# A graph layer on one core: the loop over units taken two at a time

## The chip, the cores and the metric

One core of a Trainium2 chip. The metric is the device time of one execution in microseconds (us); of several executions the median is given. Matrix products run on TensorE (PE; PEld is its weight load), elementwise work and reductions on VectorE (DVE), activations and copies on ScalarE (ACT), the issue of indirect gathers on GpSimd (POOL) and most other DMAs on SyncE (SP). PE writes its results to PSUM, which has eight banks.

## What is computed

```python
h = max(layernorm(x), 0)                     # x: 6250 nodes x 64
msg = relu(h[src] + edge_attr)               # 206250 edges x 64, sorted by dst
agg = segment_sum(msg, dst, 6250)
out = x + relu((h + agg) @ W1 + b1) @ W2 + b2
```

## The kernel before, in words

The edges are taken in groups of 768: 128 partitions with 6 columns each, one column being one edge per partition. There are 268 whole groups and a tail. A group's edge rows come by DMA (`attr_load`, tile `ea`). The rows `h[src]` come in two ways. Three columns of most groups are gathered on POOL, one indirect DMA per column (`gather`, L198, tile `xg`). The other three columns are a *unit*: they are fetched by matrix products. One group in 23 ("whole") has both halves fetched by products and no gather, so that it makes two units. The main loop has 276 units; two units are a *set*, and there are 138 sets.

For a set, three things are prepared and used:

- `found` and `backs`, zero-one matrices that DVE makes by comparisons (`find`, L446, three per set; `back`, L465, five per set; a sixth part of `backs` is made on ACT by `back_far`, L455, and `back_near`, L458). They need `sources` and `spots`, broadcast into SBUF by SP (`source_load`, `spot_load`).
- *Slots*: `slots_of` (L478) multiplies `found` with `hp`, the table of `h` rows split in three bf16 parts, into a PSUM tile `half` (three buffers, a bank each). `slots_out` (L486) copies it on ACT to `picked`. Six such fills, 104 matmuls, make a set.
- *Picks*: `pick` (L493, 18 matmuls per unit) multiplies `backs` with `picked` into one of two PSUM tiles, `pick_banks[u % 2]`. `room` (L499) has ACT copy the unit's edge columns beside them first.

`messages(u)` then adds gathered rows to edge rows on DVE (L560), which is the last reader of that `xg` buffer, sums a unit's four parts from PSUM into `ea` (L563) and applies relu on ACT (L565, tile `msg`). `one_hot` (L544) compares each edge's place in its window of 32 nodes. `window_sum` (L575) multiplies `msg` with it into a spare part of `pick_banks[u % 2]`, and `sum_into_z` (L538) adds that to `z`, the node table, on DVE.

Besides, once per six units, eight small steps rank the edges of a later chunk (`rank_at`, L272; `rank_count`, L277 and L279 on PE; `rank_of`, L285 to L291; `rank_marks`, L299; `rank_turn`, L315 on PE; `rank_holds`, L303; `rank_fits`; `source`, L329 on PE). Each unit has at most a few of them. Blocks of finished nodes go through W1 and W2 behind the loop (`hidden`, `result`, `store`).

The order on each engine is the order of the calls, written by hand; there is no scheduler. `half(u)` is one step of the loop. It does the window sum of unit u - 1, room for u + 1, three fills of slots for the next set, the picks of u + 1, the addition to `z` of u - 2, the messages and one-hots of u, and about half of a set's comparisons. The picks of a step go to the other `pick_banks` tile than the addition to `z` of that step reads:

```python
        if u + 1 < U:
            pick(u + 1, range(H))
        sum_into_z(u - LAG)
        blocks_behind(u - LAG)
        messages(u)
```

The rank steps of one chunk are a step of the loop apart where DVE and PE hand over (`rank_at` at u + 14, `rank_count` at u + 13, and so on). The gathers stand nine groups ahead (`AHEAD`), with twelve buffers.

Of the kernel before, what the change touches and what calls it, by code (L numbers as in the profile page):

```python
# [20 lines left out]
P = 128  # L21
G = 6
# [10 lines left out]
W = 32  # L33
# [48 lines left out]
def kernel(  # L82
# [296 lines left out]

    def combine(xg, ea, n):  # L380
        nc.vector.tensor_tensor(xg[:, :n], xg[:, :n], ea[:, :n], ALU.add)
        msg = work.tile([P, G, D], F32, name="msg", bufs=3)
        nc.scalar.activation(msg[:, :n], xg[:, :n], AF.Relu)
        return msg

# [75 lines left out]
    def back(k, q0, q1):  # L461
# [5 lines left out]
        if q1 == Q:  # L467
            spots.pop(k)

    def slots_of(k, n0):  # L470
        ps = psum.tile([P, 2, 3 * D], F32, name="half", bufs=3)
        for u in range(2):
            i, q = divmod(n0 + u, Q)
            sets = BB + 1 if q == 0 else BB
            for b in range(sets):
                for j in range(J):
                    m = (b * PARTS + q * J) + j if b < BB else BB * PARTS + j
                    nc.tensor.matmul(ps[j * S:(j + 1) * S, u], found[k][:, m, i, :],  # L478
                                     hp[:, min(m, RR - 1)].rearrange("p t d -> p (t d)"),
                                     start=(b == 0), stop=(b == sets - 1))  # L480
        if n0 == 0:
            picked[k] = hot.tile([P, 2 * Q, 3 * D], BF16, name="picked")
        halves[k, n0] = ps
# [17 lines left out]
    def group_of(u):  # L501
        return UNITS[u][0] if u >= 0 else F0 + u
# [14 lines left out]
    def norm_edges(xg):  # L517
        s = work.tile([P, G], F32, name="raw_s")
        nc.vector.tensor_reduce(s, xg, AX.X, ALU.add)
        nc.vector.tensor_scalar_mul(s, s, 1.0 / D)  # L520
        nc.vector.tensor_tensor(xg, xg, s.unsqueeze(2).to_broadcast([P, G, D]), ALU.subtract)
        sq = work.tile([P, G, D], F32, name="msg", bufs=3)
        nc.scalar.activation(sq, xg, AF.Square)
        fill()
        v = work.tile([P, G], F32, name="raw_v")
        nc.vector.tensor_reduce(v, sq, AX.X, ALU.add)
        nc.scalar.activation(v, v, AF.Sqrt, bias=eps_sb, scale=1.0 / D)
        fill()
        nc.vector.reciprocal(v, v)
        nc.vector.scalar_tensor_tensor(xg, xg, 0.0, v.unsqueeze(2).to_broadcast([P, G, D]),  # L530
                                       op0=ALU.max, op1=ALU.mult)

    aggs, hots, taken, msgs = {}, {}, {}, {}
    pick_banks = [psum.tile([P, H + 1, 4, D], F32, name=f"pick{i}", bufs=1) for i in range(2)]

    def sum_into_z(u):
# [3 lines left out]
    def one_hot(u):  # L540
        g, (lo, hi) = group_of(u), span(u)
        n = hi - lo
        oh = work.tile([P, G, W], F32, name="oh")
        nc.vector.tensor_tensor(  # L544
            oh[:, lo:hi], slot[:, g * G + lo:g * G + hi].unsqueeze(2).to_broadcast([P, n, W]),
            slots.unsqueeze(1).to_broadcast([P, n, W]), ALU.is_equal)
        hots[u] = oh
# [2 lines left out]
        if g <= NG and g not in taken:  # L550
            taken[g] = loaded[g] if g < RAW else load(g)

    def messages(u):
        g, (lo, hi) = group_of(u), span(u)
        ea, xg = taken[g]
        m = pool_cols(g)
        if g < RAW:
            norm_edges(xg)
        if m:
            nc.vector.tensor_tensor(ea[:, lo:m], ea[:, lo:m], xg[:, lo:m], ALU.add)  # L560
        if u >= 0:
            c0 = UNITS[u][1]
            nc.vector.tensor_reduce(ea[:, c0:c0 + H], picks.pop(u)[:, :H].rearrange("p j t d -> p j d t"), AX.X, ALU.add)  # L563
        msg = work.tile([P, G, D], F32, name="msg", bufs=3)
        nc.scalar.activation(msg[:, lo:hi], ea[:, lo:hi], AF.Relu)  # L565
        msgs[u] = msg
        if is_last(u):
            taken.pop(g)

    def window_sum(u):  # L570
        (lo, hi), oh, msg = span(u), hots.pop(u), msgs.pop(u)
# [43 lines left out]

    hid, res = {}, {}

    def blocks_behind(u):
        g = group_of(u)
        for c in sorted(res):  # L620
            store(c, *res.pop(c))
        for c in sorted(hid):
            res[c] = result(c, *hid.pop(c))
        for c in range(NB):
            if READY[c] == g and is_last(u):
                hid[c] = hidden(c)

    def chunk(i, then):
# [4 lines left out]
    def is_set(k):  # L633
        return 0 <= k < KS

    def half(u):
        g = group_of(u)
        k, i = divmod(u, 2)
        first = ((0, 2), (6, 8))[i]
        later = ((4,), (10,))[i]  # L640
        now = is_set(k + 1)
        if is_first(u):
            enter(g + AHEAD)
        if i == 0:
            if is_set(k + 3):
                source_load(k + 3)
        elif is_set(k + 3):
            spot_load(k + 3)
        window_sum(u - 1)
        if u + 1 < U:  # L650
            room(u + 1)
        if now:
            for n0 in first:
                slots_of(k + 1, n0)
                slots_out(k + 1, n0)
            for n0 in later:
                slots_of(k + 1, n0)
        if u + 1 < U:
            pick(u + 1, range(H))
        sum_into_z(u - LAG)  # L660
        blocks_behind(u - LAG)
        messages(u)
        if now:
            for n0 in later:
                slots_out(k + 1, n0)
        one_hot(u)
        if i == 0:
            if is_set(k + 1):
                back_near(k + 1)
                back(k + 1, 3, Q)  # L670
            if is_set(k + 2):
                find(k + 2, 0)
                find(k + 2, BB)
        else:
            if is_set(k + 2):
                back_far(k + 2)
                back(k + 2, 0, 3)
                find(k + 2, 1)
        chunk(u + 14, rank_at)
        chunk(u + 13, rank_count)  # L680
        chunk(u + 12, rank_of)
        chunk(u + 11, rank_marks)
        chunk(u + 11, rank_turn)
        chunk(u + 10, rank_holds)
        chunk(u + 10, rank_fits)
        chunk(u + 9, source)
        if g in CHECKS and is_first(u):
            find_left(CHECKS.index(g))

    def fill():  # L690
        while split:
# [55 lines left out]
        spot_load(k)  # L747
    for g in range(F0):
        enter(g + AHEAD)
        messages(g - F0)  # L750
        one_hot(g - F0)
        if g == 0:
            rank_at(1)
# [9 lines left out]
        if g == 3:  # L763
            rank_at(2)
            rank_count(2)
        if g >= 1:
            window_sum(g - 1 - F0)
        if g > LAG:
            sum_into_z(g - LAG - 1 - F0)
# [3 lines left out]
    ln_stack.close()  # L773
    hot = ctx.enter_context(tc.tile_pool(name="hot", bufs=2))

    for b in range(BB + 1):
        find(0, b)
    back_far(0)
    back(0, 0, Q)
    back_near(0)  # L780
    for n0 in range(0, 2 * Q, 2):
        slots_of(0, n0)
        slots_out(0, n0)
    source_load(2)
    spot_load(2)
    room(0)
    pick(0, range(H))
    for b in range(BB + 1):
        find(1, b)
    back_far(1)  # L790
    back(1, 0, 3)
    for u in range(U):
        half(u)
    xbs[NB] = old_rows(NB)
    for c in sorted(hid):
        res[c] = result(c, *hid.pop(c))
    window_sum(U - 1)
    for c in sorted(res):
        store(c, *res.pop(c))
# [78 lines left out]
```

## Time and profile before

| | |
|---|---|
| three runs | 1760.12, 1771.63, 1772.58 us; median 1771.63 |
| the profiled execution | 1747.93 us, its span 1746.2 us |
| granted PE clock, mean | 0.907 |
| busy: PE, PEld, DVE, ACT, POOL | 1302.7, 991.3, 1024.7, 871.5, 802.7 us |
| slots, L478 PE | 14352 matmuls, 500.8 us |
| picks, L493 PE | 4968 matmuls, 574.6 us |
| window sums, L575 PE | 3224 matmuls, 177.3 us |
| `half` to `picked`, L486 ACT | 828 copies, 477 ns each |
| reduces, L563 DVE | 276, 951 ns each |
| `backs`, L465 DVE | 690, 251.0 us |
| `found`, L446 DVE | 414, 212.4 us |
| one-hots, L544 DVE | 281, 341 ns each |
| first and last pick begin at | 114.3 and 1733.1 us |

Busy time is the time in which an engine had an instruction running; matmuls overlap each other, so that their sum can't be read as a rate. In a line of a timeline the numbers are start and duration in us, then engine, source line, operation, tiles, shapes and how many instructions were merged (x43); square brackets give the idle time of that engine before the line and what ended it, "issue" being nothing that the profile shows. In a line of groups the bar is followed by busy time, mean ns of one, and the idle time before them with its main reason.

### The profile page before, as it was taken

What the parts mean: (1) busy time and instruction counts of PE and PEld (TensorE: products, weight loads), DVE (VectorE), ACT (ScalarE), POOL (GpSimd) and SP (SyncE); (2) the same over time, 40 slices, a digit from 0 to 9 for tenths busy, and PEclk for the clock granted to TensorE, in tenths of its full rate; (3) what the DMA queues carried; (4) which work ended last, traced back from release to release, by engine and by line L of the source; (5) the groups of instructions that cost most, each with busy time, mean ns of one, the idle gap of its engine ahead of it and who ended that gap; (6) DMA issues with size and microseconds to landing.
All of it is one profiled execution on the core that took longest, in us unless ns stands there. A gap on an engine that the chain in (4) does not pass through costs nothing.

```text
span 1746.2 us, 54838 instructions
## 1 busy us (share of the span) xinstructions
PE 1302.7 (75%) x23181; PEld 991.3 (57%) x23181; DVE 1024.7 (59%) x2686; ACT 871.5 (50%) x1955; POOL 802.7 (46%) x798
## 2 busy tenths in 40 slices
PE   3047787778778778777777877877777877777787
PEld 2035566556557556565655655655665655565566
DVE  7346556546565665555755655654566566465576
ACT  4235455446455555554544544644554555454465
POOL 6734435444453553544544444444444445444430
PEclk9998889889897898989988988987899889898898
DMA  6223334334333442443433333333333334333341
GB/s 181 66 57 108 103 93 109 91 88 114 99 98 95 114 109 82 108 106 93 117 96 91 106 99 95 104 98 90 94 103 106 93 106 110 86 103 95 97 111 33
DMA packets 115095, 172.34 MB, mean 99 GB/s; under 512 B 28443, under 2 KB 83612, under 8 KB 114844
## 3 DMA queue, kind: packets, MB, share of 16 engines
q1 hardware_dynamic: 89752, 143.03, 27.4%
q0 software_dynamic: 25088, 25.74, 8.3%
q8 instruction: 184, 3.01, 0.7%
q14 instruction: 67, 0.55, 0.1%
q10 hardware_dynamic: 4, 0.01, 0.0%
HBM read 164.85 MB, written 3.84 MB: 97 GB/s over the span
## 4 chain that ended last, share of the span: by engine, by line
PE 64%; issue 18%; another core or an unknown queue 7%; ACT 6%; DVE 3%; POOL 1%; DMA 1%; DVEq 0%; ACTq 0%; POOLq 0%
PE pick L493 28%; PE half L478 24%; PE pick L575 8%; ACT picked L486 2%; PE rows L329 1%; ACT msg L565 1%; PE rows L592 1%; PE rows L603 1%; ACT dist L455 1%; PE rows L279 1%; POOL xg L198 1%; PE rows L277 1%; PE rows L315 0%; ACT backs L458 0%
## 5 line engine op out<-in xcount | busy, mean ns | idle before, releaser
L198 POOL DMA_INDIRECT xg<-h_rows,src_sb x754 | 768.0, 1019 | 865.4 <-DVE ea L560 688.2
L478 PE MATMUL half<-hp,found 128*32 128x192 bf16 x14352 | 500.8, 260 | 215.3 <-issue 191.8
L486 ACT CAST picked<-half 128x384 bf16<-128x384 f32 x828 | 381.1, 477 | 521.7 <-remote 321.7
L493 PE MATMUL pick<-picked,backs 128*128 128x192 bf16 x4968 | 574.6, 267 | 83.9 <-issue 64.2
L493 PEld LDWEIGHTS <-backs 128*128 128x128 bf16 x4968 | 446.6, 106 | 198.1 <-issue 179.6
L478 PEld LDWEIGHTS <-found 128*32 128x32 bf16 x14352 | 340.7, 100 | 320.7 <-issue 284.0
L538 DVE TENSOR_TENSOR z<-z,pick 128x32 f32 x281 | 53.1, 189 | 656.7 <-issue 236.4
L563 DVE TENSOR_REDUCE ea<-pick 128x192 f32<-128x768 f32 x276 | 262.5, 951 | 0.0
L465 DVE TENSOR_SCALAR backs<-spots,ids 128x768 bf16<-128x768 int16 x690 | 251.0, 415 | 0.0
L575 PE MATMUL pick<-oh,msg 128*64 128x32 f32 x3224 | 177.3, 237 | 54.6 <-ACT msg L565 29.5
L446 DVE TENSOR_SCALAR found<-sources,nodes_of 128x1536 bf16<-128x1536 int16 (+1 forms) x414 | 212.4, 542 | 0.1
L575 PEld LDWEIGHTS pick<-oh,msg 128*64 128x64 f32 x3224 | 138.4, 149 | 119.7 <-issue 53.7
L565 ACT ACTIVATE msg<-ea 128x384 f32<-128x384 f32 (+2 forms) x281 | 144.4, 514 | 24.5 <-DVE ea L563 12.8
L499 ACT COPY pick<-ea 128x192 f32<-128x192 f32 x276 | 88.6, 321 | 126.0 <-remote 69.4
L458 ACT ACTIVATE backs<-dist,ones 128x768 bf16<-128x768 bf16 x138 | 130.5, 946 | 0.3 <-ACT dist L455 0.3
L455 ACT ACTIVATE dist<-spots,far 128x768 bf16<-128x768 int16 x138 | 129.9, 941 | 0.0
L544 DVE TENSOR_TENSOR oh<-slot,slots 128x192 f32<-128x192 int16 (+2 forms) x281 | 95.7, 341 | 24.2 <-remote 24.2
L560 DVE TENSOR_TENSOR ea<-ea,xg 128x192 f32<-128x192 f32 x252 | 90.2, 358 | 3.4 <-issue 1.9
L277 PE MATMUL rows<-at,upper 128*128 128x432 f16 x46 | 17.0, 369 | 44.9 <-remote 24.1
L281 ACT CAST before<-rows 128x432 f16<-128x432 f32 x46 | 23.6, 514 | 48.4 <-remote 38.8
L332 ACT CAST source<-rows 24x64 int16<-24x64 f32 x138 | 27.6, 200 | 35.9 <-remote 27.6
L329 PE MATMUL rows<-holds,marks 128*96 128x96 f16 x276 | 27.6, 235 | 15.2 <-DVE oh L544 4.9
(102 smaller groups left out, 435.1 us busy)
## 6 DMA issues: line engine op xcount, KB each, us to landing
sources<-source_row SPq DMA_DIRECT2D x138, 384.0 KB
ea<-in_edge_attr_dram SPq DMA_DIRECT2D x268, 192.0 KB
spots<-spot_rows SPq DMA_DIRECT2D x138, 192.0 KB
xg<-h_rows,src_sb POOLq DMA_INDIRECT x754
xb<-in_x_dram SPq DMA_DIRECT2D x12, 128.0 KB
out_dram<-o SPq DMA_DIRECT2D x12, 128.0 KB
h_rows<-x SPq DMA_DIRECT2D x3, 384.0 KB
dst_sb<-in_dst_main_dram SPq DMA_DIRECT2D x1, 804.0 KB
```

Of the source, the lines that this page charges most:

```text
L198: nc.gpsimd.indirect_dma_start(out=xg[:, j, :], out_offset=None, in_=rows[:, :], in_offset=bass.IndirectOffsetOnAxis(ap=idx[:, j:j + 1], a ...
L446: nc.vector.tensor_scalar(found[k][:, b * PARTS:b * PARTS + n].rearrange("p m i s -> p (m i s)"), sources[k][:, :n * 2 * S], nodes_of[:, b ...
L455: nc.scalar.activation(dists[k], spots[k].bitcast(I16), AF.Abs, bias=far)
L458: nc.scalar.activation(backs[k][:, Q - 1].rearrange("p t s -> p (t s)"), dists.pop(k), AF.Relu, bias=ones[:, 0:1], scale=-1.0)
L465: nc.vector.tensor_scalar(backs[k][:, q].rearrange("p t s -> p (t s)"), spots[k].bitcast(I16), ids[:, q:q + 1], None, op0=ALU.is_equal)
L478: nc.tensor.matmul(ps[j * S:(j + 1) * S, u], found[k][:, m, i, :], hp[:, min(m, RR - 1)].rearrange("p t d -> p (t d)"), start=(b == 0), st ...
L486: nc.scalar.copy(picked[k][:, n0:n0 + 2], halves.pop((k, n0)))
L493: nc.tensor.matmul(ps[:, u, :3].rearrange("p t d -> p (t d)"), backs[k][:, q, i * H + u, :], picked[k][:, i * Q + q], start=(q == 0), stop ...
L544: nc.vector.tensor_tensor(oh[:, lo:hi], slot[:, g * G + lo:g * G + hi].unsqueeze(2).to_broadcast([P, n, W]), slots.unsqueeze(1).to_broadca ...
L563: nc.vector.tensor_reduce(ea[:, c0:c0 + H], picks.pop(u)[:, :H].rearrange("p j t d -> p j d t"), AX.X, ALU.add)
L565: nc.scalar.activation(msg[:, lo:hi], ea[:, lo:hi], AF.Relu)
L575: nc.tensor.matmul(pa[i * D:(i + 1) * D], msg[:, j, :], oh[:, j, :], start=(j < lo + 2), stop=(j >= hi - 2))
```

## The change

The step of the loop is now a set, `both(k)`, with units 2k and 2k + 1. The two window sums come first (of the set before), then the sums by node (`messages` is split in `total` and `relu`; the reduce now stands ahead of the addition of gathered rows), with room for the next set's units and six fills of slots, then two relus, the picks of both units of the next set, both additions to `z`, both one-hots, and all comparisons for the set two ahead. `msg` gets four buffers for three, `oh` four for two. The two SP loads of a set stand together. The rank steps of both units stand at the end of the step. Ahead of the loop, set 1 gets all of its comparisons and set 0 both of its picks.

```diff
+    def backs_of(k):
+        back_far(k)
+        back(k, 0, Q)
+        back_near(k)
...
-        oh = work.tile([P, G, W], F32, name="oh")
+        oh = work.tile([P, G, W], F32, name="oh", bufs=4)
...
-    def messages(u):
+    def total(u):
         g, (lo, hi) = group_of(u), span(u)
         ea, xg = taken[g]
         m = pool_cols(g)
-        if g < RAW:
-            norm_edges(xg)
-        if m:
-            nc.vector.tensor_tensor(ea[:, lo:m], ea[:, lo:m], xg[:, lo:m], ALU.add)
         if u >= 0:
             c0 = UNITS[u][1]
             nc.vector.tensor_reduce(ea[:, c0:c0 + H], picks.pop(u)[:, :H].rearrange("p j t d -> p j d t"), AX.X, ALU.add)
-        msg = work.tile([P, G, D], F32, name="msg", bufs=3)
-        nc.scalar.activation(msg[:, lo:hi], ea[:, lo:hi], AF.Relu)
-        msgs[u] = msg
+        if m:
+            nc.vector.tensor_tensor(ea[:, lo:m], ea[:, lo:m], xg[:, lo:m], ALU.add)
+        totals[u] = ea
         if is_last(u):
             taken.pop(g)
+
+    def relu(u):
+        lo, hi = span(u)
+        msg = work.tile([P, G, D], F32, name="msg", bufs=4)
+        nc.scalar.activation(msg[:, lo:hi], totals.pop(u)[:, lo:hi], AF.Relu)
+        msgs[u] = msg
...
-    def half(u):
...
+    def both(k):
+        us = (2 * k, 2 * k + 1)
+        ahead = is_set(k + 1)
+        for u in us:
+            if is_first(u):
+                enter(group_of(u) + AHEAD)
+        if is_set(k + 3):
+            source_load(k + 3)
             spot_load(k + 3)
+        for u in us:
+            window_sum(u - 2)
+        for u in us:
+            total(u)
+            if ahead:
+                room(u + 2)
+                for n0 in range(u % 2 * Q, u % 2 * Q + Q, 2):
+                    slots_of(k + 1, n0)
+                    slots_out(k + 1, n0)
+        for u in us:
+            relu(u)
+        if ahead:
+            for u in us:
+                pick(u + 2, range(H))
+        for u in us:
+            sum_into_z(u - 2)
+        blocks_behind([u - 2 for u in us])
+        for u in us:
+            one_hot(u)
+        if is_set(k + 2):
+            backs_of(k + 2)
+            for b in range(BB + 1):
+                find(k + 2, b)
+        for u in us:
+            chunk(u + 14, rank_at)
+            chunk(u + 13, rank_count)
+            chunk(u + 12, rank_of)
+            chunk(u + 11, rank_marks)
+            chunk(u + 11, rank_turn)
+            chunk(u + 10, rank_holds)
+            chunk(u + 10, rank_fits)
+            chunk(u + 9, source)
...
-    for u in range(U):
-        half(u)
+    for k in range(KS):
+        both(k)
```

## The prediction

> **What bounds the kernel now.** I read the chain of waits and the groups of instructions first, then the timeline of single units, then the order of the changed program.
>
> From the chain (first line) and the groups:
>
> ```profile
> PE 64%; issue 18%; another core or an unknown queue 7%; ACT 6%; DVE 3%; POOL 1%; DMA 1%; DVEq 0%; ACTq 0%; POOLq 0%
> ...
> L198 POOL DMA_INDIRECT xg<-h_rows,src_sb x754 | 768.0, 1019 | 865.4 <-DVE ea L560 688.2
> ...
> L538 DVE TENSOR_TENSOR z<-z,pick 128x32 f32 x281 | 53.1, 189 | 656.7 <-issue 236.4
> ```
>
> PE carries the chain, with 18% in which it waits for nothing that shows ("issue"). DVE has slack: 656.7 us of it stand ahead of the addition to z, once per unit. POOL's gathers wait for the addition of edge and gathered rows (L560), which frees their buffer.
>
> Where the 18% goes, in one unit at granted clock 1.00:
>
> ```profile
> 820.04 0.19 DVE L538 TENSOR_TENSOR z<-z,pick 128x32 f32 x1 [2.43 <-ACT msg L565]
> 820.17 0.36 DVE L560 TENSOR_TENSOR ea<-ea,xg 128x192 f32<-128x192 f32 x1
> 820.27 0.54 PE L575 MATMUL pick<-oh,msg 128*64 128x32 f32 x12
> 820.45 0.95 DVE L563 TENSOR_REDUCE ea<-pick 128x192 f32<-128x768 f32 x1
> 820.74 1.09 PE L478 MATMUL half<-hp,found 128*32 128x192 bf16 x43
> 820.80 0.94 POOL L198 DMA_INDIRECT xg<-h_rows,src_sb  x1 [1.82 <-DVE ea L560]
> 822.14 0.27 PE L478 MATMUL half<-hp,found 128*32 128x192 bf16 x2 [0.32 <-issue]
> 822.88 0.33 PE L478 MATMUL half<-hp,found 128*32 128x192 bf16 x5 [0.47 <-issue]
> 823.62 0.29 PE L478 MATMUL half<-hp,found 128*32 128x192 bf16 x2 [0.42 <-issue]
> 823.85 0.34 PE L493 MATMUL pick<-picked,backs 128*128 128x192 bf16 x2
> 824.39 0.49 PE L493 MATMUL pick<-picked,backs 128*128 128x192 bf16 x4 [0.21 <-issue]
> 825.15 1.15 PE L493 MATMUL pick<-picked,backs 128*128 128x192 bf16 x12 [0.27 <-issue]
> ```
>
> The gathers start 0.27 us after L560. Some 43 matmuls later PE falls into steps of 0.75 us with 2 to 6 matmuls each, until 0.77 us after the third gather's end (824.38). I call it the stutter: 58 matmuls from 820.80 to 825.15. The last units have no gathers left:
>
> ```profile
> 1724.19 0.54 PE L575 MATMUL pick<-oh,msg 128*64 128x32 f32 x12
> 1724.67 1.26 PE L478 MATMUL half<-hp,found 128*32 128x192 bf16 x52
> 1725.86 1.66 PE L493 MATMUL pick<-picked,backs 128*128 128x192 bf16 x18
> 1727.44 0.54 PE L575 MATMUL pick<-oh,msg 128*64 128x32 f32 x12
> ```
>
> There a unit takes 3.25 us, against (1733.4 - 114.3) / 276 = 5.87 us over the loop. So the loop is bound by PE plus the stutter. A longer burst, six gathers in a row, is in the trace too:
>
> ```profile
> 456.74 1.04 POOL L198 DMA_INDIRECT xg<-h_rows,src_sb  x1 [6.28 <-DVE oh L544]
> ...
> 463.18 0.95 POOL L198 DMA_INDIRECT xg<-h_rows,src_sb  x1 [0.30 <-issue]
> ...
> 463.97 0.29 PE L478 MATMUL half<-hp,found 128*32 128x192 bf16 x4 [1.14 <-issue]
> 465.39 0.69 PE L478 MATMUL half<-hp,found 128*32 128x192 bf16 x12 [1.14 <-issue]
> ```
>
> From 456.74 to 465.39, 8.65 us, PE gets through 68 matmuls by the timeline's counts, less than two trios pass in that time.
>
> **The change, part by part.** Counts of matmuls, comparisons, copies and gathers stay. Extra buffers (msg, oh) cost nothing in time; the prologue gains one unit's picks and part of a set's comparisons, at most 18 x 0.088 + 3 x 0.364 + 0.95 = 3.6 us. SP issues a set's two loads together, three sets ahead; they have a whole set of cover.
>
> The added wait decides. In both(k), sum_into_z(u-2) stands behind pick(u+2), and both use pick_banks[u % 2]. In the changed program as built, DVE's additions to z wait for the last matmul of pick(u+2), of the very set in hand. Before, the pick they waited for was the preceding step's. Queued behind them on DVE: two one-hots, five backs, three finds, the rank steps, then the next set's reduces and L560 additions. Who waits for that:
> - PE: the rank product (L315, L329 or L277, one per set) now follows the set's picks and waits for a DVE rank step of the same set; the next window sums and slots stand behind it.
> - ACT: room(u+2) waits for the next reduce and stands ahead of slots_out; with three half buffers PE gets through three of six banks and stops.
> - POOL: the gathers wait for the L560 additions.
>
> So a set becomes a loop. From T, the end of a set's picks, at full clock:
> 1. z 0.10 after T, 0.19; one-hots 2 x 0.341; backs 251.0 / 690 x 5 = 1.82; finds 212.4 / 138 = 1.54: T+4.3.
> 2. Rank steps, one of three kinds per set: L285, L288, L291 (0.377 + 0.603 + 0.180), L303 (0.55) or L272 (0.45), mean 0.72: T+5.0. PE's product 0.57 on average with 0.1 to start, then the first window sums 0.54 and 0.1: T+6.3.
> 3. First reduce to T+7.25; L560 ends at T+7.5; gathers from T+7.8; second reduce to T+8.4.
> 4. room 0.32, then copies 0.43 apart: the three banks are free at T+8.1, 8.5 and 8.95. PE does the other 52 slot matmuls behind them, to T+9.5.
> 5. 36 picks at 1.58 / 18 = 0.088: T+12.7.
>
> That is already more than 11.72 us per set (1617.5 / 138 from 115.9 to 1733.4). The stutter comes on top, and nothing hides it now: six gathers start at T+7.8, and steps 4 and 5 (88 matmuls) run under them. What the stutter lets through is not shown for this mix. By the burst of six it is 68 in 8.65 us, to T+16.45: 20 picks are left, 1.76 us: **18.2**. By the rate between the gaps in bursts of three (median 4.4 matmuls per us over 170 of them, counted in the timeline) it is 52 + 29 by T+16, and T+16.6. I take the first, since the burst has the same length. With one trio in a set: 58 by T+12.15 to 13.4, 24 to 30 picks left: 15.2.
>
> 754 / 3 = 252 units (rounded) have gathers, 24 have none: 114 sets of 18.2 and 24 of 15.2, mean 17.7; x 138 = 2440. With 114 us ahead of the first pick, 13 behind the last and 3.6 of prologue: 2570 against the span of 1746.2. The profiled run's whole time was 1747.93; the median of the three runs, 1771.63, is 1.0136 times that: **2600**.
>
> Clock: from 869 to 873 PE was busy 1.43 of 4.00 us, and from 873.5 to 880.5 the granted clock averaged 0.52. At half clock picks take 2.19 / 13 = 0.168 and twelve window matmuls 0.86 instead of 0.54. PE now has nothing to do from T to T+5.1. If that halves the clock each time, leftover picks cost 1.6 to 2.2 us more and a set 0.3 elsewhere: mean 19.7 per set, 2880. I keep it as the upper end, for stretches as idle as the stutter often left the clock at 1.00 (820 to 826: 1.00). The Trainium skill ("TensorE: Matmul & The Clock Gate", section on HAM oscillation) says that idle gaps over about 3.4 us put the clock to half. By that rule the sum is this 2880, and these rows agree in part.
>
> **The rivals.**
> - *The loop of waits without the stutter*: PE, having waited, holds enough ready work to get through 88 matmuls. For: it ran about 43 to 53 before the first gap. Against: 88 is more. 12.7 per set: 138 x 12.7 + 130 = 1883, x 1.0136 = 1908; with 36 picks and the window sums at half clock (2.9 + 0.3 more per set) 2360. The Trainium skill ("Runtime: NRT & Kernel Launch", section "Instruction fetch mechanics") has PE's instructions streamed ahead and hidden, which would leave no stutter: its time is this 1908. The gaps during gathers speak against it.
> - *Faster*: one burst of six falls on window sums and picks, and the 84 slot matmuls that are left run unhindered. This decides if DVE's work after the picks fits under window sums and slots, about 3.3 us, or PE needn't wait for it: 8.2 us for 80 matmuls and 84 x 0.024 = 2.0, 10.3 per set, 138 x 10.3 + 130, x 1.0136 = 1570. Against: step 1 alone is 4.3 us, and ACT's order holds three banks back.
> - *No change*: waits shrink until the old 11.7 per set returns. Nothing in the order does that.
>
> **How the numbers follow.** Forecast 0.75 (2360 to 2880), first rival 0.17 (1900 to 2360), faster 0.05, no change 0.03. Within 1% is about what a measurement of this kernel tells from none. The range goes from 1900, to hold the first rival, to 2880.
>
> **What would show it.** Right: z's idle time ended by PE's pick, and that idle before the additions, with DVE idle during picks and PE idle after them; PE's window sums or rank product ended by DVE; bursts of six gathers of 7.5 us; PE's busy share near 50%; a lower granted clock. Wrong: gaps of "issue" gone while POOL gathers (first rival), or window sums starting within 1 us of the last pick (then the loop of waits isn't there, and the time is near or below the old one).

## The result, and the profile after

| | before | after |
|---|---|---|
| median (lowest to highest), six runs each | 1763.01 us (1737.17 to 1772.58) | 2901.42 us (2897.99 to 2907.06) |
| the profiled execution, its span | 1747.93, 1746.2 us | 2904.16, 2902.4 us |
| granted PE clock, mean | 0.907 | 0.731 |
| busy: PE, DVE, POOL | 1302.7, 1024.7, 802.7 us | 1663.3, 1019.8, 747.1 us |

The ratio is 1.6601, with an interval of 1.65 to 1.6703; it is taken over the fast runs alone, which are three of the six before, so it is not the quotient of the two medians. The forecast was 2600 us with a range of 1900 to 2880, so the measured time lies 0.7% above the range's upper end, on the forecast side and by a larger amount than forecast.

Line numbers have moved: slots are now L483, picks L498, the copies to `picked` L491, the addition to `z` L543, the one-hots L549, the addition of gathered rows L566, the window sums L582. The page's busy times and groups of the changed kernel (busy us, mean ns of one, then idle time ahead of the group and what ended most of it):

```profile
PE 1663.3 (57%) x23181; PEld 1317.5 (45%) x23181; DVE 1019.8 (35%) x2686; ACT 909.0 (31%) x1955; POOL 747.1 (26%) x798
...
L198 POOL DMA_INDIRECT xg<-h_rows,src_sb x754 | 713.1, 946 | 2044.6 <-DVE ea L566 1854.3
L483 PE MATMUL half<-hp,found 128*32 128x192 bf16 x14352 | 754.5, 337 | 571.9 <-issue 520.3
...
L543 DVE TENSOR_TENSOR z<-z,pick 128x32 f32 x281 | 53.0, 189 | 1697.2 <-PE pick L498 1615.3
...
L498 PE MATMUL pick<-picked,backs 128*128 128x192 bf16 x4968 | 626.1, 305 | 17.9 <-issue 17.0
...
L315 PE MATMUL rows<-ident_b,spot_i 128*18 128x128 bf16 x46 | 12.0, 260 | 226.0 <-DVE spot_i L291 226.0
L329 PE MATMUL rows<-holds,marks 128*96 128x96 f16 x276 | 28.2, 246 | 191.0 <-DVE holds L303 182.1
L277 PE MATMUL rows<-at,upper 128*128 128x432 f16 x46 | 19.2, 418 | 201.5 <-DVE at L272 195.0
```

Of these, the page of the kernel before has:

```profile
L478 PE MATMUL half<-hp,found 128*32 128x192 bf16 x14352 | 500.8, 260 | 215.3 <-issue 191.8
L493 PE MATMUL pick<-picked,backs 128*128 128x192 bf16 x4968 | 574.6, 267 | 83.9 <-issue 64.2
...
L277 PE MATMUL rows<-at,upper 128*128 128x432 f16 x46 | 17.0, 369 | 44.9 <-remote 24.1
...
L329 PE MATMUL rows<-holds,marks 128*96 128x96 f16 x276 | 27.6, 235 | 15.2 <-DVE oh L544 4.9
```

DVE's idle time ahead of the addition to `z` went from 656.7 to 1697.2 us, and 1615.3 us of it now end with a pick. PE in turn loses 226.0 + 182.1 + 195.0 = 603 us ahead of the three rank products, each time to a DVE step; before, it stood idle there for 12.7 us (L315), 15.2 us (L329) and 44.9 us (L277), and mostly waited for something else. So the two engines wait for each other in turn, once per set. PE's other idle time is nearly all "issue" ahead of slots, 520.3 us against 191.8; picks, which had 64.2 us of it before, have 17.0.

One set of the timeline (start, duration, engine, line; square brackets: idle time before, and what ended it):

```profile
1514.86 0.19 DVE L543 TENSOR_TENSOR z<-z,pick 128x32 f32 x1 [1.28 <-PE pick L498]
...
1515.50 1.73 DVE L465 TENSOR_SCALAR backs<-spots,ids 128x768 bf16<-128x768 int16 x5
1517.14 1.34 DVE L446 TENSOR_SCALAR found<-sources,nodes_of 128x1536 bf16<-128x1536 int16 x3
...
1519.00 0.56 PE L329 MATMUL rows<-holds,marks 128*96 128x96 f16 x6 [4.24 <-DVE holds L303]
1519.49 1.40 PE L582 MATMUL pick<-oh,msg 128*64 128x32 f32 x24
...
1520.82 3.28 PE L483 MATMUL half<-hp,found 128*32 128x192 bf16 x82
...
1522.50 0.95 POOL L198 DMA_INDIRECT xg<-h_rows,src_sb  x1 [14.17 <-DVE ea L566]
...
1524.56 0.34 PE L483 MATMUL half<-hp,found 128*32 128x192 bf16 x5 [0.45 <-issue]
...
1526.73 0.37 PE L483 MATMUL half<-hp,found 128*32 128x192 bf16 x4 [0.47 <-issue]
...
1528.75 0.95 POOL L198 DMA_INDIRECT xg<-h_rows,src_sb  x1 [0.30 <-issue]
...
1529.63 0.38 PE L483 MATMUL half<-hp,found 128*32 128x192 bf16 x4 [0.39 <-issue]
...
1531.06 5.85 PE L498 MATMUL pick<-picked,backs 128*128 128x192 bf16 x36 [1.05 <-issue]
...
1537.00 0.19 DVE L543 TENSOR_TENSOR z<-z,pick 128x32 f32 x1 [2.61 <-PE pick L498]
```

Read from the first line to the last, this is the loop: the addition to `z` waits for the picks, then DVE works through comparisons while PE stands idle for 4.24 us, then window sums and slots start, then six gathers run in a row from 1522.50 to 1529.70, and PE crawls through slots in steps of one to five matmuls until 1531.06. Only then do the 36 picks of the set run, all of them, and DVE waits for their end.

The same set cut into its three stretches (columns: length, busy us of PE, PEld, DVE, ACT and POOL with instructions, granted clock, DMA share, GB/s):

```profile
1514.80:1522.50 7.70, 3.50 (x74) 3.33 (x77) 7.54 (x21) 1.08 (x5) 0.00 (x0) 0.81 0.09 19
1522.50:1531.00 8.50, 4.15 (x68) 1.92 (x61) 0.87 (x2) 1.90 (x5) 5.67 (x6) 0.70 0.62 165
1531.00:1537.00 6.00, 5.85 (x36) 5.24 (x35) 0.19 (x1) 1.69 (x4) 0.00 (x0) 0.52 0.10 33
```

In the first stretch DVE is busy nearly throughout (7.54 of 7.70 us) and PE less than half. In the second POOL gathers, DVE mostly stands, and PE is busy for half of it. In the third PE works nearly alone, at a granted clock of 0.52.

For the numbers below: on some occasions the chip showed no stutter at all, and the kernel before then took 1102 to 1104 us with all its gathers, so that a time is only to be read beside that of the kernel before in the same group. Where the changed kernel did not run in a group, its 2901.42 us stand in for it below; over the three groups in which it ran, its time differed by 1.2%.

### The profile page after: what moved, and what is told of

Its sections match the earlier page's. It is cut to its first block, busy times and chain, and to the rows that moved or that the text cites. A ratio compares the mean times of both kernels' runs of the same rounds, so it can differ in the third digit from the quotient of the medians.

```text
span 2902.4 us, 54486 instructions
## 1 busy us (share of the span) xinstructions
PE 1663.3 (57%) x23181; PEld 1317.5 (45%) x23181; DVE 1019.8 (35%) x2686; ACT 909.0 (31%) x1955; POOL 747.1 (26%) x798
## 3 DMA queue, kind: packets, MB, share of 16 engines
q1 hardware_dynamic: 89752, 143.03, 16.8%
q0 software_dynamic: 25088, 25.74, 4.7%
## 5 line engine op out<-in xcount | busy, mean ns | idle before, releaser
L198 POOL DMA_INDIRECT xg<-h_rows,src_sb x754 | 713.1, 946 | 2044.6 <-DVE ea L566 1854.3
L483 PE MATMUL half<-hp,found 128*32 128x192 bf16 x14352 | 754.5, 337 | 571.9 <-issue 520.3
L483 PEld LDWEIGHTS <-found 128*32 128x32 bf16 x14352 | 510.8, 129 | 776.7 <-issue 714.0
L543 DVE TENSOR_TENSOR z<-z,pick 128x32 f32 x281 | 53.0, 189 | 1697.2 <-PE pick L498 1615.3
L491 ACT CAST picked<-half 128x384 bf16<-128x384 f32 x828 | 374.6, 482 | 865.6 <-remote 512.0
L498 PE MATMUL pick<-picked,backs 128*128 128x192 bf16 x4968 | 626.1, 305 | 17.9 <-issue 17.0
L498 PEld LDWEIGHTS <-backs 128*128 128x128 bf16 x4968 | 568.6, 124 | 82.5 <-issue 59.2
L465 DVE TENSOR_SCALAR backs<-spots,ids 128x768 bf16<-128x768 int16 x690 | 238.7, 413 | 0.0
L582 PE MATMUL pick<-oh,msg 128*64 128x32 f32 x3224 | 189.0, 282 | 3.4 <-DVE oh L549 3.4
L446 DVE TENSOR_SCALAR found<-sources,nodes_of 128x1536 bf16<-128x1536 int16 (+1 forms) x414 | 184.6, 501 | 0.1
L582 PEld LDWEIGHTS pick<-oh,msg 128*64 128x64 f32 x3224 | 170.3, 205 | 30.9 <-issue 19.1
L315 PE MATMUL rows<-ident_b,spot_i 128*18 128x128 bf16 x46 | 12.0, 260 | 226.0 <-DVE spot_i L291 226.0
L329 PE MATMUL rows<-holds,marks 128*96 128x96 f16 x276 | 28.2, 246 | 191.0 <-DVE holds L303 182.1
L277 PE MATMUL rows<-at,upper 128*128 128x432 f16 x46 | 19.2, 418 | 201.5 <-DVE at L272 195.0
L574 ACT ACTIVATE msg<-ea 128x384 f32<-128x384 f32 (+2 forms) x281 | 129.4, 515 | 7.7 <-DVE ea L566 7.3
L329 PEld LDWEIGHTS <-marks 128*96 128x96 f16 x276 | 26.4, 158 | 199.0 <-issue 164.1
L315 PEld LDWEIGHTS <-spot_i 128*18 128x18 bf16 x46 | 4.1, 90 | 239.8 <-DVE spot_i L291 239.8
```

What stands on the lines that cost most here:

```text
L198: nc.gpsimd.indirect_dma_start(out=xg[:, j, :], out_offset=None, in_=rows[:, :], in_offset=bass.IndirectOffsetOnAxis(ap=idx[:, j:j + 1], a ...
L446: nc.vector.tensor_scalar(found[k][:, b * PARTS:b * PARTS + n].rearrange("p m i s -> p (m i s)"), sources[k][:, :n * 2 * S], nodes_of[:, b ...
L465: nc.vector.tensor_scalar(backs[k][:, q].rearrange("p t s -> p (t s)"), spots[k].bitcast(I16), ids[:, q:q + 1], None, op0=ALU.is_equal)
L491: nc.scalar.copy(picked[k][:, n0:n0 + 2], halves.pop((k, n0)))
L498: nc.tensor.matmul(ps[:, u, :3].rearrange("p t d -> p (t d)"), backs[k][:, q, i * H + u, :], picked[k][:, i * Q + q], start=(q == 0), stop ...
L574: nc.scalar.activation(msg[:, lo:hi], totals.pop(u)[:, lo:hi], AF.Relu)
```

## The experiments

Times are medians where there were several runs. Each group of kernels ran together with the kernel before on one chip, and the time of the kernel before on that chip is given beside them.

**Both kernels again.** The unedited kernels were timed on another chip, and the changed one on a further one.

> The kernel before, unchanged, run and traced once more, since beside the two runs with the late additions it took 1102 us and not 1763. If PE's stutter under gathers is a property of the kernel, 1737 to 1773 us with the gaps of issue. If it is a condition of the machine that comes and goes between loads of a program, either that, or 1102 us with gathers running and no gaps, which is the time of the kernel without gathers (1103 us).

> The changed kernel, unchanged, beside it. With the stutter about 2901 us. Without it the loop of waits through DVE alone is left, and the time is that of the changed kernel without gathers, about 1966 us, slower than the kernel before by the factor 1.78.

> The changed kernel as it is, to see its time beside a kernel before of known state. If the kernel before shows the gaps (1735 to 1765 us): 2860 to 2910. If it shows none (about 1103 us): by the theory that the loss is the loop of waits plus the gaps, about the 1966 us that it took without gathers; by the rival that gathers cost the changed kernel something of their own apart from the gaps, over 2050.

The kernel before took 1735.41 us (ratio to its companions 1.0008, 0.9958 to 1.0058), the changed one 2867.25 (1.6546, 1.6415 to 1.6676) and 2868.34 beside 1731.7. The size of the loss holds in all three groups. All three met the stutter, so the time of the changed kernel on a chip without it stays unmeasured.

**No gathers.** In both kernels the gathers of the loop are left out and a zeroed tile stands in their place; all else stays.

```diff
         else:
-            xg = edge.tile([P, G - H, D], F32, name="xg")
+            return ea, none
         gather(...)
...
+    none = const.tile([P, G - H, D], F32, name="none")
+    nc.vector.memset(none, 0.0)
```

> The changed kernel without the gathers of the main loop (a tile of zeros is added in place of the gathered rows; all else runs). Theory: the loop of waits alone is left, 12.7 us per set at full clock to 15.9 at half clock: 1880 to 2320 us, and no gaps of issue of 0.4 us and more in the slots. Rival (the stutter has nothing to do with the gathers): over 2700 us with the gaps in place.

> The kernel before without the gathers of the main loop (zeros added in place of the gathered rows). Theory: each unit takes the 3.25 us of the last units of the trace, 6.5 us per set and about 1030 us in all. Rival (the gaps of issue come from PE's own stream of instructions): 1600 us or more, gaps in place.

The changed kernel took 1965.67 us, the kernel before 1103.28 (about 1030 were expected), beside 1764.86 for the kernel before as it is. So 662 us of the kernel before are owed to its gathers (1764.86 - 1103.28), and 936 us of the changed kernel (2901.42 - 1965.67). What is left, 1965.67 - 1103.28 = 862 us, is the price of the waits, with the lower clock that goes with them (0.762 against 0.968). The timeline of the changed kernel without gathers shows them with nothing in the way:

```profile
995.70 3.14 PE L500 MATMUL pick<-picked,backs 128*128 128x192 bf16 x36
1003.77 0.22 PE L317 MATMUL rows<-ident_b,spot_i 128*18 128x128 bf16 x1 [4.92 <-DVE spot_i L293]
1003.92 1.26 PE L584 MATMUL pick<-oh,msg 128*64 128x32 f32 x24
1005.11 3.53 PE L485 MATMUL half<-hp,found 128*32 128x192 bf16 x104
1008.58 3.14 PE L500 MATMUL pick<-picked,backs 128*128 128x192 bf16 x36
```

PE is idle for 4.92 us after the picks, and then the 104 slots and 36 picks run without one gap of "issue". From pick to pick this set takes 1008.58 - 995.70 = 12.88 us, and the sets 13.6 on average. The prediction's loop without stutter has 12.7.

**The addition to `z` ahead of the picks.** One edit of the changed kernel, called the early-additions kernel below: both additions stand right behind the window sums.

```diff
         for u in us:
             window_sum(u - 2)
+        for u in us:
+            sum_into_z(u - 2)
         for u in us:
             total(u)
...
-        for u in us:
-            sum_into_z(u - 2)
```

> The changed kernel with both additions to z moved ahead of the sums by node, so that they wait for the window sums and not for the set's picks; nothing is left out. Theory (two parts: a loop of waits through DVE, and PE's stutter under a burst of six gathers): the loop is cut, DVE's comparisons fall beside slots and picks, z's idle time is no longer ended by PE's pick. The burst of six stays and starts about 2.8 us after the picks' end, so a set takes 13.2 to 15.6 us and the kernel 1950 to 2280 us, still slower than the kernel before. Rival (the loop of waits alone makes the loss): 11.7 us or less per set, 1760 us or less. Rival (the burst alone makes it): over 2700 us.

> The changed kernel with the additions to z moved ahead of the sums by node, beside it. With the stutter about 2157 us. Without it about 1276 us, its time without gathers: the loop of waits is cut, and what is left over the kernel before (1102 us) is about 174 us of waits in the middle of the slots.

It took 2156.51 us, and 2126.35 in another group (ratio 1.227, 1.2181 to 1.2359). That is 745 us less than the changed kernel's 2901.42, and 741 less than the 2867.25 that the changed kernel took beside the second: two thirds of the 1138 us that the change lost (2901.42 - 1763.01). The timeline says why:

```profile
1202.74 0.89 PE L582 MATMUL pick<-oh,msg 128*64 128x32 f32 x24
1203.56 1.26 PE L483 MATMUL half<-hp,found 128*32 128x192 bf16 x52
1205.75 1.17 PE L483 MATMUL half<-hp,found 128*32 128x192 bf16 x45 [0.94 <-ACT picked L491]
```

Window sums and slots now follow at once. What PE waits for next is the copy of a bank (`picked`), because `room` stands ahead of it on ACT and waits for DVE's reduce. Over the whole run this wait is 120.0 us; 419.5 us more are "issue" ahead of slots and picks.

The same kernel with the gathers left out as above:

> The kernel z_early without the gathers of the main loop (zeros added in place of the gathered rows). Theory: what is left of a set is PE's 6.5 us and the wait of about 0.9 us for a free half buffer in the middle of the slots, so 7.4 us per set and 1100 to 1200 us; the difference from z_early's 2157 us, about 1000 us, is then the price of 754 gathers in bursts of six, against 1764.9 - 1103.3 = 662 us for the same gathers in bursts of three. Rival (z_early is slow by some other wait in its order): over 1500 us.

1276.34 us, above what was expected. So 173 us of waits are left (1276.34 - 1103.28) that the early addition does not remove; and its gathers cost 2156.51 - 1276.34 = 880 us, against 662 us for the same 754 gathers in the kernel before.

**The rank steps moved apart.** The changed kernel, its late additions kept, with the rank steps put so that each product of PE uses a DVE step of an earlier set.

```diff
-            chunk(u + 14, rank_at)
-            chunk(u + 13, rank_count)
-            chunk(u + 12, rank_of)
+            chunk(u + 18, rank_at)
+            chunk(u + 15, rank_count)
+            chunk(u + 14, rank_of)
...
-            chunk(u + 10, rank_holds)
-            chunk(u + 10, rank_fits)
+            chunk(u + 12, rank_holds)
+            chunk(u + 12, rank_fits)
...
+        if g == 4:
+            rank_of(2)
```

> The changed kernel with the rank steps spread so that each of PE's rank products stands one set behind the DVE step that feeds it; nothing is left out. Theory (PE's window sums and slots stand behind the rank product, which waits for the end of DVE's comparisons): window sums start about 1 us after the picks' end in place of about 5, all of the first three banks of slots are done when the gathers start, about 10 more matmuls are ahead of the burst; 1.5 to 2.6 us per set less, 2540 to 2700 us. Rival (the rank product hides behind the wait for the half buffers): within 2% of the changed kernel, about 2900 us.

2498.18 us beside 1764.86: 403 us better than the changed kernel, a little more than expected, and still far from the kernel before. The rank products no longer wait, but the slots behind them do:

```profile
1221.87 1.50 PE L582 MATMUL pick<-oh,msg 128*64 128x32 f32 x24 [0.70 <-DVE oh L549]
1224.23 0.35 PE L483 MATMUL half<-hp,found 128*32 128x192 bf16 x4 [0.86 <-DVE found L446]
1224.76 2.15 PE L483 MATMUL half<-hp,found 128*32 128x192 bf16 x48 [0.18 <-DVE found L446]
```

The comparisons that the next step's slots need end only after this step's picks, because they stand behind the addition to `z`. Slots wait 150.2 us for `found` in this kernel, by its list of PE's waits, against 6.8 us in the changed one, where the wait for the rank product stands ahead and hides it.

**What in a gather makes the stutter.** The kernel before with each gather of the loop replaced by a plain DMA of as many rows, without indices, issued from POOL or from SP. The rows are the wrong ones for the sum; bytes, buffers and waits stay.

```diff
-        gather(xg[:, lo:], src_sb[:, g * G + lo:g * G + hi], hi - lo, x if g < RAW else h_rows)
+        if g < F0:
+            gather(...)
+        else:
+            for j in range(lo, hi):
+                nc.gpsimd.dma_start(out=xg[:, j, :], in_=h_rows[j * P:(j + 1) * P, :])
```

> The kernel before with each gather of the main loop replaced by a plain DMA of 128 whole rows of h (fixed rows, so the sums are other sums), still issued by POOL. Asks what of a gather makes PE stutter. If it is POOL's issue of a DMA: 1600 us or more with the gaps of issue in place. If it is the indexed form of the gather: 1100 to 1250 us without gaps.

> The same plain DMAs issued by SP in place of POOL. If the bytes moved or their landing in SBUF make PE stutter: 1600 us or more. If it is POOL's work: 1100 to 1250 us without gaps.

> The plain DMAs from POOL in place of the gathers, once more, beside kernels with gathers, as no kernel with gathers ran beside it the first time. If the indexed gathers are what PE's stutter needs: about 1100 us while the kernel before takes 1712 to 1773 us. If the traffic does it too: 1600 us or more.

From POOL 1100.39 us, from SP 1096.84, and from POOL in another group 1106.2 beside 1756.45 (0.6274, 0.62 to 0.6348). These are the times without any gather. In the kernel with POOL's plain DMAs POOL still issues 754 of them, by its groups of instructions:

```profile
L225 POOL DMA_DIRECT2D xg<-h_rows x754 | 467.3, 631 | 525.3 <-DVE ea L564 504.0
```

The DMA table of that page has the same 25088 packets and 25.74 MB on the queue of POOL's DMAs (q0) as that of the kernel with gathers. So neither the bytes nor the packets nor the issue of DMAs on POOL holds PE up. It takes the indexed gather. The plain DMAs read rows that lie side by side, so whether it is the index or the scattered rows was not separated.

**Where and how the gathers stand.** The kernel before, with the addition of gathered rows and the relu moved behind the one-hots, or behind the comparisons, so that gathers start at another place of the unit.

```diff
+    def messages_end(u):
+        ...
+        if m:
+            nc.vector.tensor_tensor(ea[:, lo:m], ea[:, lo:m], xg[:, lo:m], ALU.add)
+        msg = ...
...
         one_hot(u)
+        messages_end(u)
```

> The kernel before with the addition of gathered rows (L560) and the relu behind it moved after the unit's reduce and one-hot, so that each burst of three gathers starts about 2.0 us after the picks' end in place of 0.87, when the 52 slot matmuls of that unit are done. Nothing is left out. Theory (a burst lets through a number of matmuls, not a time of them, so it should meet the long picks and leave the short slots outside): a unit takes 5.0 to 5.3 us in place of 5.87, 1510 to 1600 us. Rival (the place of a burst in the unit does not matter): within 2% of the kernel before. Second rival (bursts run into each other and become bursts of six): slower than before.

> The same with the addition and relu moved further, after the unit's share of comparisons, so that a burst starts about 3.4 us after the picks' end. Theory: 5.0 to 5.3 us per unit, 1510 to 1600 us, as the burst now meets the window sums and part of the slots of the next unit after 43 matmuls of grace. Rival (the place does not matter): within 2% of the kernel before. Second rival (relu comes too late for the window sums, PE waits for ACT): slower than the kernel with the addition after the one-hot.

> The kernel before with the addition of gathered rows moved after the one-hot, once more, as its first runs met a machine in which the kernel before did not stutter (1102 us). If it stutters now (the kernel before at 1712 to 1773 us): by the theory that a burst lets through a number of matmuls, 1510 to 1600 us; by the rival that the burst's place in a unit does not matter, within 2% of the kernel before. If it does not stutter, 1110 us again and nothing new.

The first two met a chip without the stutter: 1110.5 us beside 1102.21 (1.0069, 1.0042 to 1.0096) and 1220.75 (1.1062, 1.1027 to 1.1098), the second because the relu comes too late for the window sums (PE waits 114.8 us for it there). On a chip with the stutter the first took 1935.43 us beside 1756.45 (1.0952, 1.0826 to 1.1079). The expected 1510 to 1600 us did not come, but the idea that a later start would let a unit's slots escape was not tried by itself, since the bursts have joined: the trace has 40 of six gathers in a row (at most 0.4 us apart) and 157 of three, where that of the kernel before has 6 and 225.

That made the number of gathers in a row the next suspect. The early-additions kernel was changed so that only the first unit's buffer comes free before the picks; the addition and the relu of the second unit stand behind the comparisons.

```diff
     def relu(u):
         lo, hi = span(u)
+        if u >= 0 and u % 2:
+            m = pool_cols(group_of(u))
+            if m:
+                ea, xg = totals[u], gathered.pop(u)
+                nc.vector.tensor_tensor(ea[:, lo:m], ea[:, lo:m], xg[:, lo:m], ALU.add)
...
-        for u in us:
-            relu(u)
+        relu(us[0])
...
             for b in range(BB + 1):
                 find(k + 2, b)
+        relu(us[1])
```

> The kernel z_early with the second unit's addition of gathered rows and relu moved after the set's comparisons, so that the six gathers of a set come as two bursts of three with a pause. With the stutter: if the loss of z_early (2126 to 2157 us) comes from bursts of six, which let through 62 to 68 matmuls where two of three let through 58 each, a set takes 10.5 to 12.5 us in place of 14.5, 1600 to 1860 us. If the number of gathers counts and not their grouping, within 2% of z_early. Without the stutter: about 1280 us.

1757.64 us beside 1756.45 (1.0039, 0.9998 to 1.008): 369 to 399 us less than the early-additions kernel (2126.35 and 2156.51), and no different from the kernel before. The trace has 237 bursts of three and none of six, where that of the early-additions kernel has 107 of six. One unit's addition and relu moved with the split, so the 369 us can't be put down to the bursts alone.

**Room behind the first copies.** The largest wait left in the kernel with the split was the one for a bank. Its list of PE's waits (instruction, what it waited for, us in all, times, longest):

```profile
PE half L483 <- ACT picked L491: 147.2, 118, 4.8
PE half L483 <- issue: 135.0, 308, 1.2
PE pick L498 <- issue: 51.7, 192, 0.7
```

The rooms were put behind the first three copies.

```diff
-            if ahead:
-                room(u + 2)
-                for n0 in range(u % 2 * Q, u % 2 * Q + Q, 2):
-                    slots_of(k + 1, n0)
-                    slots_out(k + 1, n0)
+        if ahead:
+            for n0 in range(0, 2 * Q, 2):
+                if n0 == Q:
+                    for u in us:
+                        room(u + 2)
+                slots_of(k + 1, n0)
+                slots_out(k + 1, n0)
```

> The kernel z_early_split with both rooms moved behind the first three copies of slots, so that those copies no longer wait on ACT behind a room that waits for a reduce. Nothing is left out. Theory: the wait of about 1 us for a free half buffer in the middle of the slots goes, and with the stutter a set takes 10.7 to 11.2 us in place of 11.7, 1610 to 1690 us against 1712 to 1773 us for the kernel before. Rival (the time that PE no longer waits is lost again under the burst, which lets through a fixed number of matmuls): within 2% of the kernel before. Without the stutter: about 1140 us against 1102 us.

> The kernel with the early additions to z, split bursts and both rooms behind the first three fills, once more, on whatever the kernel before does beside it. If the kernel before shows the gaps (1735 to 1765 us): z_early_split took 1757.64 there; the rooms were in the way of slots_out only while ACT waited for the second reduce, under 1 us per set, so 1650 to 1760 by the theory that ACT's order still costs something, and 1760 or more by the rival that the wait for DVE behind the picks (a rank step, 0.8 us of idle PE per set without gaps) sets the end anyway. If the kernel before shows no gaps (about 1103 us): 1282 again, within 1%.

On a chip without the stutter it took 1281.75 us beside 1103.84 (1.1643, 1.1607 to 1.1678), more than expected. On one with the stutter it took 1639.45 us beside 1731.7: ratio 0.9452, 0.9385 to 0.9519, somewhat better than the theory's lower end of 1650. Its list of PE's waits:

```profile
PE half L483 <- issue: 106.7, 257, 1.2
PE rows L315 <- DVE spot_i L291: 60.1, 37, 5.4
PE pick L498 <- issue: 48.9, 159, 1.7
...
PE half L483 <- ACT picked L491: 1.1, 4, 0.3
```

The 147.2 us for a bank are 1.1 us, and the wait for the rank step, 6.3 us with the split alone, takes back 60.1. This version beats both kernels where the stutter is present. Where it is absent it takes 16% longer than the kernel before.

## Where the prediction was right, and where it was wrong

**Right: before is bound by PE plus the stutter.** Without the gathers PE is busy for 91% of the span, with no group that has more than 1 us of "issue" ahead of slots or picks, and 662 of 1765 us go.

**Right: the added wait and the loop.** The additions to `z` wait for the set's own picks, comparisons queue behind them, and PE's rank product waits for those. Moving the additions alone took away two thirds of the loss. The signs named ahead are there: DVE idle under the picks and PE behind them, bursts of 7.2 us (1522.50 to 1529.70; 7.5 were forecast), and PE busy for 57% of the span where about 50% was forecast.

**Right in size: the loop without the stutter.** 12.7 us per set and 1908 us in all were forecast for that rival, 2360 at half clock; the kernel without gathers took 13.6 us per set and 1965.67 us in all, at a granted clock of 0.762. As a rival it fell, since the gaps stayed. The Trainium skill ("Runtime: NRT & Kernel Launch", section "Instruction fetch mechanics") has instructions streamed ahead with the fetch mostly hidden. By that the time would have been this one; the 520.3 us of "issue" ahead of slots speak against taking it as a rule for PE while POOL gathers, though no run shows that the fetch is what holds PE up.

**Wrong: the term for picks under the burst.** The prediction had 52 of a set's 104 slots done when the burst starts, held there by the banks. Of the other 88 matmuls, 68 pass in the 8.65 us from the burst's start, 52 slots and 16 picks, and 20 picks are left at 0.088 us. The trace has 106 sets with six gathers in a row (the loop's first set left out):

| from the end of a set's picks | predicted | measured, mean |
|---|---|---|
| to the first gather | 7.8 us | 7.41 us |
| first gather to the first pick | | 9.35 us |
| first pick to the end of the last | | 4.69 us |
| these two together | 8.65 + 1.76 = 10.41 us | 14.04 us |
| the set | 18.2 us | 21.45 us |

When the burst began, 28 slots had started in 97 of the 106 sets, not 52, so that 76 were still ahead. (The set shown above is one of the exceptions, with 44.) The banks did not hold them: PE's waits for `picked` ahead of slots are 1.9 us in the whole run. The slots had only just begun, and at half clock. This is the time from the first slot to the first gather in the next set (length, busy us of PE and PEld with instructions of L483, granted clock, DMA share, GB/s):

```profile
1543.55:1544.52 0.97, 0.97 (x28) 0.96 (x32) 0.50 0.77 143
```

That is 0.035 us for a slot, where the forecast reckons with 0.024. What a burst lets through was nearly right: in the median 63 matmuls start in the 8.65 us from the first gather, against 68. But they were slots. About 13 slots and all 36 picks were left behind the burst, not 20 picks, and a pick took 4.69 / 36 = 0.130 us, not 0.088. So what was left took 14.04 - 8.65 = 5.39 us where 20 x 0.088 = 1.76 were forecast, 3.63 us more; the burst starts 0.39 us earlier than forecast, and the rest is the 3.25 us by which the set is longer. At the forecast's own prices, 13 slots and 36 picks are 13 x 0.024 + 36 x 0.088 = 3.48 us, so that by this estimate about half of the miss is the count of what was left and half its lower rate.

The sets with fewer gathers were too short in the forecast as well: the 22 with three took 16.8 us where 15.2 were forecast. The six behind the last gather took 11.3 us.

**Too low: the clock.** The sum was made at full clock, with half clock as its upper end. The granted clock was 0.731 on average, 0.52 in the stretch of picks above. The Trainium skill ("TensorE: Matmul & The Clock Gate", section on HAM oscillation) ties a halved clock to idle gaps over about 3.4 us. The changed kernel has one such gap in most sets (4.24 us above), and by that rule the sum was 2880. That 2901 us are so near is in part luck, since that sum keeps the 20 picks and prices them at 0.168 us, 3.4 us in all, where 13 slots and 36 picks took 5.39. A single long gap isn't needed, either. In the kernel with the rank steps apart no idle time of PE from 1221 to 1239 us is longer than 0.9 us, and the granted clock is 0.50 throughout, by the same columns as the stretches above:

```profile
1221.00:1230.00 9.00, 6.43 (x128) 5.19 (x127) 6.97 (x18) 2.06 (x6) 1.95 (x3) 0.50 0.21 74
1230.00:1239.00 9.00, 6.87 (x39) 4.73 (x38) 0.19 (x1) 3.80 (x7) 3.71 (x4) 0.50 0.09 18
```

The traces show what does go with it. In the loop of the changed kernel the granted clock is 0.50 or 1.00 for pieces of 3.41 us: it went up only behind a piece in which PE was busy for 80% or more of the time, and down only behind one with 63% or less (247 times each). In the kernel with the rank steps apart, PE is busy for 60 to 77% of each such piece from 1222.6 to 1236.3 us, and the clock stays down. No experiment separates the clock's share of the loss from that of the gaps.

**Overlooked: the comparisons as a second wait.** The prediction put PE's wait on the rank product alone. It cost nothing in the forecast, as the rank product is the later of the two, but it made the rank steps look like the one thing to move, and moving them recovered 403 us, not the 603 that PE loses there.

**The rival on the other side** (1570 us) asked that DVE's work behind the picks fit under window sums and slots, or that PE not wait for it. Neither holds in the changed kernel: PE waits 4 to 5 us. The kernel that came near to it, with early additions, split bursts and late rooms, meets its second condition in most sets, and took 1639.45 us. The scaling by 1.0136 from the profiled execution to the median had no counterpart after the change, 2904.16 us profiled and 2901.42 in the median; without it the forecast would have been 2570, further off.

**The account.** Of the 1138 us lost, 862 are waits with their lower clock (the two kernels without gathers), and about 936 - 662 = 274 are what gathers cost beyond their price before, in bursts of six instead of three. This split holds for taking the gathers out first; waits and gathers act on each other.

## What to carry to other kernels

When an order written by hand is regrouped, look for each read of a shared PSUM tile that has moved behind the next write to it: the tile's wait turns a pipeline into a loop, and the price is all that is queued behind the waiting instruction, on its engine and on those that wait for that. A fix for the first wait in such a loop should be priced against the second, which it uncovers: here the comparisons behind the rank steps, the bank behind the additions to `z`, and the rank step behind the rooms. Buffers that come free together make transfers start together, and where those slow another engine, spreading the releases is worth a try: here it came with 369 us, against 741 for the early additions, though a moved addition and relu had a part in it.

## What the runs showed of the hardware that was not expected

The stutter belongs to indexed gathers and to a condition that comes and goes. The kernel before took 1102.21 us on one occasion and 1764.86 on another, on the same chip and with the same gathers. Without the stutter PE ran through them without a gap:

```profile
602.03 1.26 PE L478 MATMUL half<-hp,found 128*32 128x192 bf16 x52
603.22 1.66 PE L493 MATMUL pick<-picked,backs 128*128 128x192 bf16 x18
```

This is the kernel with the addition behind the one-hots, and gathers of 1.03 to 1.30 us each ran one behind the other, 0.30 us apart, all through those 2.85 us. What sets the condition is open.

ACT is held up as well, or at least waits for something that the profile can't name ("remote"). Ahead of its copies to `picked`, in the kernel before and in the changed one:

```profile
ACT picked L486 <- remote: 321.7, 147, 6.2
```

```profile
ACT picked L491 <- remote: 512.0, 179, 5.8
```

In the kernels without gathers, with plain DMAs, and with gathers but no stutter, that row is absent; there the copies wait for PE's slots almost alone, 4.8 to 145.4 us in all. Some of it may be PE's own delay under another name. What inside an indexed gather reaches the other engines was not shown.
